# Last layer norm of a four-layer graph network on one Trainium2 core: its scaling on ScalarE, its rows in the ten shared row buffers

## The chip, the cores and the metric

The kernel runs on one core of one Trainium2 chip. A core has a matrix engine (TensorE, PE in the profile), three engines that work element by element (VectorE = DVE, ScalarE = ACT, GpSimd = POOL), a queue engine that issues transfers (SyncE = SP), and 16 DMA engines that move data between the chip's memory and the on-chip memory. The engines run side by side and each takes its own instructions strictly in order; an instruction that has to wait holds back everything behind it on its engine. The metric is the device time of one execution in microseconds; lower is better.

## What is computed

There are 16 graphs of 1024 nodes with 128 features. Four layers follow each other, each of the form `x = layernorm(x + layer(x))`. The change concerns the end of the fourth. That layer is three SAGE convolutions with batch norms, whose three results are concatenated and multiplied by one matrix; the sum with the layer's input is then normalised per node:

```python
xc = jnp.concatenate([h1, h2, h3], axis=-1) * mf[..., None]
return (xc @ Wl + bl) * mf[..., None]
...
m = jnp.mean(x, axis=-1, keepdims=True)
v = jnp.var(x, axis=-1, keepdims=True)
x = (x - m) / jnp.sqrt(v + eps)
```

## The kernel before

Layers 0 to 2 and the preparation of layer 3 take the first 5340 us or so. Their instructions are placed by hand under `tc.manual_schedule`. Layer 3 is written as plain loops over graphs, and the order in which its instructions stand in each engine's queue is chosen by the program's own scheduler: a load can stand in SP's queue well ahead of its place in the source.

Layer 3 has four passes over the 16 graphs, since each batch norm needs the sums over all graphs before the next convolution can be scaled.

- Passes 1 and 2 convolve. `expanded` (L934 to L938) converts a graph's edges from one byte to four, into eight tiles named `m` of 128x1024 numbers each. All `m` tiles share ten buffers (`bufs=10`). The convolution L950 reads them.
- Pass 3 (`second`, then `columns`) makes the third result. `second` (L1089) loads what the convolution left in memory into a tile named `h`, of which there are two buffers. Here the `m` buffers are not used for edges any more.
- Pass 4, the last, is the one that the change touches. It consists of `summed` and the loop behind it.

In pass 4, each tile of a graph holds 512 KB. For graph b, `summed(b)` takes two of the ten `m` buffers and loads the first and second hidden results of the graph into them (L1120); the third still lies on the chip as `R3[b]`. TensorE multiplies the three by the scaled weight (L1125, twelve matmuls of 128x512), and ScalarE moves the sum from PSUM into `o` with the bias added (L1127). The loop calls `summed(b + 1)` before it finishes graph b. To finish graph b, it takes one of the two `h` buffers for `xb` and loads the layer's input rows into it (L1134). TensorE transposes `o` back into rows, four tiles per half graph (L1138); VectorE multiplies by the node mask and adds the input, in place in `xb` (L1140, eight instructions of 128x128). Then comes `layernorm(xb, xb)`:

- VectorE takes the statistics of each of the eight row tiles (L205).
- GpSimd makes the factors from them in ten small instructions (`norm_factors`, L219 to L228; one of them, L227, is a power).
- GpSimd applies them, `x * rs + mean`, in eight instructions of 128x128 (`norm_rows`, L211). (`mean` holds minus the mean times `rs` by then.)

Last, SP issues the store of `xb` to the output (L1143). The load L1134, the loads L1120 and the store L1143 all stand in SP's queue. An `h` buffer is free for the next graph but one when its store has landed.

Layer 0 to 2 have a helper, `norm`, that applies the same factors by ScalarE (L270), so the trace shows that instruction.

Of the kernel before, what the change touches and what calls it, by code (L numbers as in the profile page):

```python
# [29 lines left out]
F32 = mybir.dt.float32  # L30
# [4 lines left out]
AF = mybir.ActivationFunctionType  # L35
# [4 lines left out]
B, N, D, H2 = 16, 1024, 128, 256  # L40
P = 128
T = N // P
# [29 lines left out]
def tile_graph_layers(ctx: ExitStack, tc, a, out):  # L72
    nc = tc.nc
# [5 lines left out]
    small = ctx.enter_context(tc.tile_pool(name="small", bufs=3))  # L79
# [87 lines left out]
    for b in range(B):  # L167
        q, g = divmod(b, G)
        nc.gpsimd.dma_start(out=half_rows[g * R:(g + 1) * R, :, q],
                            in_=a["nodemask"][b].rearrange("(k r) -> r k", r=R))  # L170
# [31 lines left out]
    def layernorm(dst, src):  # L202
        st = small.tile([P, T, 6], F32, name="ln_st")
        for t in range(T):
            nc.vector.bn_stats(out=st[:, t, :], in_=src[:, t, :])  # L205
        norm_rows(dst, src, st)

    def norm_rows(dst, src, st):
        rs, mean = norm_factors(st)
        for t in range(T):  # L210
            nc.gpsimd.tensor_scalar(dst[:, t, :], src[:, t, :], rs[:, t:t + 1], mean[:, t:t + 1],  # L211
                                    op0=ALU.mult, op1=ALU.add)

    def norm_factors(st):

        mv = small.tile([P, 4, T], F32, name="ln_mv")
        mean, apart, var, rs = (mv[:, i, :] for i in range(4))
        gp = nc.gpsimd
        gp.tensor_add(mean, st[:, :, 1], st[:, :, 4])  # L219
        gp.tensor_sub(apart, st[:, :, 1], st[:, :, 4])  # L220
        gp.tensor_scalar(mean, mean, -0.5, 0.0, op0=ALU.mult, op1=ALU.add)
        gp.tensor_mul(apart, apart, apart)
        gp.tensor_add(var, st[:, :, 2], st[:, :, 5])
        gp.tensor_scalar(var, var, 1.0 / D, LN_EPS, op0=ALU.mult, op1=ALU.add)
        gp.tensor_scalar(apart, apart, 0.25, 0.0, op0=ALU.mult, op1=ALU.add)
        gp.tensor_add(var, var, apart)
        gp.tensor_tensor(rs, var, mhalf, op=ALU.pow)  # L227
        gp.tensor_mul(mean, mean, rs)  # L228
        return rs, mean
# [653 lines left out]
    def rows_bank(name):  # L883
        return psum.tile([P, 4, D], F32, tag="subset", name=name, bufs=2)
# [48 lines left out]
    def expanded(near):  # L933
        m = []  # L934
        for c in range(T):
            m.append(sb.tile([P, N], F32R, name="m", bufs=10))
            nc.scalar.copy(m[c], near[:, c, :])  # L937
        return m  # L938
# [129 lines left out]
    sb = ctx.enter_context(tc.tile_pool(name="sb", bufs=1))  # L1068
# [5 lines left out]
    for b in range(B):  # L1074
# [3 lines left out]
        m = expanded(ahead[b][0])  # L1078
# [37 lines left out]
    def summed(b):  # L1116
        hs = []
        for l in range(2):
            r = sb.tile([P, N], F32, name="m", bufs=10)
            nc.sync.dma_start(out=r, in_=hidden[l][b])  # L1120
            hs.append(r)
        p = wide("pl")
        for s in halves:
            for l, r in enumerate((*hs, R3[b])):
                nc.tensor.matmul(p[:, s], scaled[l], r[:, s], start=(l == 0), stop=(l == 2))  # L1125
        o = sb.tile([P, N], F32, name="o", tag="sq", bufs=2)
        nc.scalar.activation(o, p, AF.Identity, bias=pl)  # L1127
        return o

    o = summed(0)  # L1130
    for b in range(B):
        following = summed(b + 1) if b + 1 < B else None
        xb = sb.tile([P, T, D], F32, name="h", bufs=2)
        nc.sync.dma_start(out=xb, in_=x3[b])  # L1134
        for h in range(2):
            p = rows_bank("pback")
            for t in range(4):
                nc.tensor.transpose(p[:, t, :], o[:, (4 * h + t) * P:(4 * h + t + 1) * P], ident)  # L1138
            for t in range(4):
                nc.vector.scalar_tensor_tensor(xb[:, 4 * h + t, :], p[:, t, :], nm[:, 4 * h + t, b:b + 1],  # L1140
                                               xb[:, 4 * h + t, :], op0=ALU.mult, op1=ALU.add)
        layernorm(xb, xb)
        nc.sync.dma_start(out=out[b].rearrange("(t p) d -> p t d", p=P), in_=xb)  # L1143
        o = following

# [24 lines left out]
```

## Time and profile before

| what | us |
|---|---|
| median of three runs (6604.93 to 6620.51) | 6616.69 |
| the profiled execution | 6613.2 |
| its span, first to last instruction | 6611.5 |
| end of VectorE's batch norm statistics aggregate, the last one ahead of pass 4's sums | 6446.4 |
| first transpose back into rows of pass 4 (L1138) | 6457.2 |
| last store issued (L1143) | 6607.3 |

The profiled execution's time is 1.7 us above its span. The span is counted from the first to the last instruction, and all times with two decimals below are read from it. Pass 4 is only the last 2.4% of the span, so the shares of the whole page say nothing about it: PE 86%, DVE 80%, ACT 56% and POOL 58% are averages over all layers. What counts here is the stretch from about 6452 us on.

A row of a view by time reads: start, duration, engine, line, operation, output from input, shapes, how often; in brackets, how long the engine had been idle before it and what ended the wait. A row of the waits reads: who waited, for whom, total us, times, longest.

### The profile page before, as it was taken

To read this page: it belongs to the slowest core of one execution; us is meant where nothing else is said; L and a number is where in the kernel's file an instruction comes from. 1 tells how busy PE (TensorE), PEld (TensorE's weight loads), DVE (VectorE), ACT (ScalarE), POOL (GpSimd) and SP (SyncE) were. 2 spreads that over 40 slices of the span, in tenths; PEclk is the share of its full clock that TensorE was granted. 3 is DMA by queue.
4 is the path that set the end of the run, shared out by engine and by line. 5 is a ranking of instruction groups with operands and counts; after the bars stand their busy time and mean duration, and the time that the engine had idled before them with its cause. 6 is when DMAs were issued, how large, how long until landed. Compare 5 with 4: busy or idle time off the path is not lost. (4 is left out here: it accounts for less than half of the span.)

```text
span 6611.5 us, 85916 instructions
## 1 busy us (share of the span) xinstructions
PE 5697.7 (86%) x27306; PEld 2883.8 (44%) x27306; DVE 5317.7 (80%) x8130; ACT 3733.9 (56%) x6537; POOL 3844.7 (58%) x11285
## 2 busy tenths in 40 slices
PE   6989898989898989899888898888888768787986
PEld 3434344444444444444444444444443345555643
DVE  3989899999999999999999999999998834444453
ACT  4656566666666666666666656666655523333841
POOL 2675767676767776766666676767676511110126
PEclk8989898989898989898989899999987779888997
DMA  5121212121212121212112212121110156563635
GB/s 37 14 27 22 30 24 36 20 27 26 28 28 27 27 27 26 28 26 31 28 29 30 27 26 27 26 27 28 25 25 9 32 93 120 105 124 102 230 128 166
DMA packets 478381, 317.02 MB, mean 48 GB/s; under 512 B 301162, under 2 KB 429668, under 8 KB 473828
## 3 DMA queue, kind: packets, MB, share of 16 engines
q0 software_dynamic: 105648, 84.20, 14.6%
q1 hardware_dynamic: 367600, 226.13, 11.7%
q8 instruction: 214, 3.51, 0.2%
q10 hardware_dynamic: 4676, 1.19, 0.1%
q14 instruction: 243, 1.99, 0.1%
HBM read 412.71 MB, written 117.18 MB: 80 GB/s over the span
## 5 line engine op out<-in xcount | busy, mean ns | idle before, releaser
L831 DVE TENSOR_TENSOR best<-best,pg 128x1024 f32<-128x1024 f32 x2720 | 3234.4, 1210 | 309.0 <-PE pg L779 300.5
L749 ACT ACTIVATE hot<-pm,one_less 128x512 fp32r<-128x512 f32 x2752 | 1882.3, 688 | 1115.1 <-PE pm L748 1102.9
L779 PE MATMUL pg<-hot,high 64*128 64x512 f32 x5504 | 1479.1, 534 | 453.6 <-DVE best L831 417.8
L779 PE MATMUL pg<-hot,low 64*128 64x512 f32 x5504 | 1173.3, 423 | 0.0
L748 PE MATMUL pm<-AT,lit 120*128 120x512 fp8e4 x2752 | 1143.8, 416 | 9.3 <-ACT hot L749 6.2
L779 PEld LDWEIGHTS pg<-hot,high 64*128 64x128 f32 x5504 | 547.9, 196 | 1265.1 <-DVE best L831 792.4
L616 POOL TENSOR_SCALAR sc<-low_counts,half_mask,rest 16x1 f32<-16x1 f32 x992 | 435.7, 439 | 399.6 <-DVE rest L603 305.8
L779 PEld LDWEIGHTS pg<-hot,low 64*128 64x128 f32 x5504 | 573.4, 205 | 0.0
L748 PEld LDWEIGHTS <-lit 120*128 120x128 fp8e4 x2752 | 274.5, 100 | 624.8 <-issue 560.8
L621 POOL TENSOR_SCALAR sc<-sc 16x1 f32<-16x1 f32 x992 | 430.1, 434 | 105.0
L770 ACT CAST low<-pt 128x256 fp32r<-128x256 f32 x688 | 255.6, 371 | 396.3 <-PE pt L768 392.1
L980 POOL TENSOR_TENSOR length<-length,mhalf 128x8 f32<-128x8 f32 x48 | 78.9, 1644 | 571.7 <-DVE length L979 571.7
L618 POOL TENSOR_SCALAR sc<-sc 16x1 f32<-16x1 f32 x992 | 341.8, 345 | 107.7
L624 POOL TENSOR_SCALAR last_rank<-V,sc 16x31 f32<-16x31 bf16 (+30 forms) x992 | 387.1, 390 | 0.0
L623 POOL TENSOR_SCALAR hit<-V,sc 16x31 bf16<-16x31 bf16 (+30 forms) x992 | 372.5, 376 | 0.0
L768 PE MATMUL pt<-high,less 128*128 128x256 f32 x688 | 303.2, 441 | 66.3 <-ACT high L763 58.9
L467 DVE TENSOR_TENSOR sub<-sub,q 128x24 f32<-128x24 f32 (+11 forms) x768 | 306.6, 400 | 24.6 <-ACT q L289 10.5
L619 POOL TENSOR_SCALAR sc<-sc 16x1 f32<-16x1 f32 x992 | 270.1, 272 | 83.3
L937 ACT CAST m<-near 128x1024 fp32r<-128x1024 fp8e4 x256 | 253.3, 1044 | 112.7 <-DVE near L906 59.8
L760 PE MATMUL pt<-ident,sub 128*128 128x128 f32 x1376 | 293.9, 298 | 24.7 <-ACT hot L749 22.0
L377 PE MATMUL pav<-v,eT 128*128 128x128 f32 x2048 | 307.6, 296 | 2.1 <-ACT eT L370 2.1
L617 POOL TENSOR_SCALAR sc<-sc 16x1 f32<-16x1 f32 x992 | 256.6, 259 | 86.6
(258 smaller groups left out, 9495.7 us busy)
## 6 DMA issues: line engine op xcount, KB each, us to landing
removed<-gone SPq DMA_DIRECT2D x128, 256.0 KB
An<-in_adj_dram POOLq DMA_DIRECT2D x16, 1024.0 KB, 15.1
E<-in_adj_dram POOLq DMA_DIRECT2D x128, 128.0 KB, 6.8
gone_all<-removed POOLq DMA_DIRECT2D x64, 256.0 KB, 12.1
near<-in_adjT_dram POOLq DMA_DIRECT2D x16, 1024.0 KB, 17.3
h<-x SPq DMA_DIRECT2D x32, 512.0 KB
kept<-near SPq DMA_DIRECT2D x16, 1024.0 KB
share<-share SPq DMA_DIRECT2D x32, 512.0 KB
```

The costliest lines, as they stand in the source:

```text
L377: nc.tensor.matmul(pav, eT[:, c, :], values[b][:, c, :], start=(c == 0), stop=(c == T - 1))
L467: nc.vector.tensor_max(sub[:, :n_g, n:2 * n], sub[:, :n_g, 0:n], qg[:, 2 * g0:2 * g0 + n_g, k:k + 1].to_broadcast([P, n_g, n]))
L616: gp.tensor_scalar(half, mine, half_mask[:, m], rest[:, n:n + 1], op0=ALU.mult, op1=ALU.add)
L618: gp.tensor_scalar(sf, half, 5.5, sf, op0=ALU.is_gt, op1=ALU.mult)
L621: gp.tensor_scalar(to, at, sf, none, op0=ALU.subtract, op1=ALU.subtract)
L623: gp.tensor_scalar(hit[:, n, n + 1:], V[:, n, n + 1:], at, None, op0=ALU.is_equal)
L624: gp.tensor_scalar(last[:, n + 1:], V[:, n, n + 1:], to, None, op0=ALU.is_le)
L748: nc.tensor.matmul(pm, lit[:, r, :], AT[b * (T + 1) + c][:, halves[h]], start=True, stop=True)
L749: nc.scalar.activation(hots[s][:, halves[h]], pm, AF.Relu, bias=one_less)
L768: nc.tensor.matmul(pt, less, high, start=False, stop=True, skip_group_check=True)
L779: nc.tensor.matmul(pg[:, a], part[rows, at * P:(at + 1) * P], hots[s][rows, halves[h]], start=(k == 0), stop=(k == 1))
L831: nc.vector.tensor_max(own, own, pg)
```

## The change

The rows of a graph, `xb`, come from the ten buffers that `m` tiles use, under the name `xb`, in place of the two that `h` tiles use. In the last layer norm the statistics (VectorE) and the factors (GpSimd) stay as they are, and the eight instructions that apply the factors go from GpSimd to ScalarE, with the same arithmetic. The number of buffers and the memory they take are the same as before. Pass 3 keeps the two `h` buffers for itself.

```diff
     for b in range(B):
         following = summed(b + 1) if b + 1 < B else None
-        xb = sb.tile([P, T, D], F32, name="h", bufs=2)
+        xb = sb.tile([P, T, D], F32, name="xb", tag="m", bufs=10)
         nc.sync.dma_start(out=xb, in_=x3[b])
 ...
-        layernorm(xb, xb)
+        st = small.tile([P, T, 6], F32, name="ln_st")
+        for t in range(T):
+            nc.vector.bn_stats(out=st[:, t, :], in_=xb[:, t, :])
+        rs, mean = norm_factors(st)
+        for t in range(T):
+            nc.scalar.activation(xb[:, t, :], xb[:, t, :], AF.Identity, bias=mean[:, t:t + 1], scale=rs[:, t:t + 1])
         nc.sync.dma_start(out=out[b].rearrange("(t p) d -> p t d", p=P), in_=xb)
```

## The prediction

> **What bounds the kernel now.** I read the page, found that the change lies in the last 2.4% of the span, and asked for the waits of that stretch alone (6452 us to the end), then the chain of waits inside it.
>
> ```profile
> ACT o L1127 <- PE pl L1125: 116.4, 16, 11.6
> DVE h L1140 <- DMA h<-x: 65.4, 11, 9.2
> POOL ln_mv L219 <- DVE ln_st L205: 43.0, 12, 14.2
> ...
> PE pback L1138 <- DVE h L1140: 31.3, 11, 8.5
> ```
>
> See the second line: VectorE's add L1140 stood still for 65.4 us because the input rows had not come. TensorE waits behind it in turn (last line), since the transposes need the PSUM banks that L1140 empties. Why the rows are late is in the chain that ended last:
>
> ```profile
> 6564.17 3.22 DMA out_dram<-h
> 6567.40 3.43 DMA h<-x
> 6570.95 2.16 DVE h L1140 x8
> 6573.11 1.57 DVE ln_st L205 x8
> ...
> 6576.55 1.64 POOL ln_mv L227
> 6578.27 0.21 POOL ln_mv L228
> 6578.57 3.48 POOL h L211 x8
> 6582.07 3.21 DMA out_dram<-h
> ```
>
> It is a ring. The store of one graph lands (3.2 us), only then is the next load into the same buffer issued (3.4), then come the add (2.16), the statistics (1.57), the factors (6574.75 to 6578.47, about 3.8 with the hand-over), the scaling on GpSimd (3.48) and the store again. From store to store, 6564.17 to 6582.07, that is 17.9 us, and with two buffers two graphs go round in it: 8.95 us a graph. Further forward, where hidden results are still being loaded, the ring is 20.2 us (stores at 6507.17 and 6527.40).
>
> Next I looked for what would bound it without the ring. By time, TensorE's first graphs, which run before the ring closes, show its own pace:
>
> ```profile
> 6457.23 1.04 PE L1138 MATMUL pback<-ident,o 128*128 128x128 f32 x8
> ...
> 6463.26 1.04 PE L1138 MATMUL pback<-ident,o 128*128 128x128 f32 x8
> ...
> 6469.28 1.04 PE L1138 MATMUL pback<-ident,o 128*128 128x128 f32 x8
> ```
>
> Three starts 6.03 and 6.02 us apart: TensorE takes 6.03 us a graph, with no gap between. In the same place GpSimd starts L219 at 6461.66 and, never idle in between, again at 6469.17: 7.51 us a graph, of which the scaling is 3.47. VectorE needs 2.16 + 1.63 = 3.8. For the transfers I took the busy times of the stretch:
>
> ```profile
> 6452.00:6611.50 159.50, 108.75 (x309) 53.63 (x307) 59.46 (x256) 17.82 (x16) 108.28 (x288) 0.81 0.53 172
> ```
>
> The columns are length, busy us of PE, PEld, DVE, ACT, POOL, then the granted clock, the DMA share and GB/s. A share of 0.53 is 84.5 us of full use, for 22 hidden loads, 14 row loads and 16 stores of 512 KB each: 1.63 us a transfer. A graph has four: 6.5 us. ACT has 17.82 us of work in 159.5.
>
> **What the Trainium skill says.** "ScalarE: Activation LUTs", section What ACT_TABLE_LOAD costs, gives 280 + 0.833 N ns for an activation with a pointer as bias, 93 more for each further pointer, and 93 of overlap between neighbours. For N = 128 and two pointers that is 480 ns and a pitch of 387. The same instruction in this trace (L270) has a median of 486 ns and eight take 3.18 us, so the page and the trace agree, and I use the trace:
>
> ```profile
> 5338.50 3.18 ACT L270 ACTIVATE X<-y,ln_mv 128x128 f32<-128x128 f32 x8 [10.64 <-POOL ln_mv L228]
> ```
>
> "DMA: Bandwidth & Descriptors", section Anatomy of one DMA, says that DMA engines don't wait on semaphores; the issuing sequencer does. The trace agrees: SP itself stood 33.9 us in 14 waits of L1134 for stores to land, and everything behind stood with it. "TensorE: Matmul & The Clock Gate", section What's actually happening, says that after some 3.4 us of idleness the matrix clock drops to half. Here the granted clock is 0.55 in 6496 to 6500 after a wait of 3.4 us, and L1125's longest matmul is 1.2 us against a median of 0.59. So the ring also costs TensorE speed, which comes back if the ring goes.
>
> **The change part by part.**
>
> *Rows in the ten buffers.* One graph now takes three of ten buffers (two hidden, one of rows), so ten hold 3.3 graphs, where before the rows stood two graphs deep and the hidden results five. A hidden buffer is held about 5 us while it loads and some 5 us while TensorE works; a row buffer 5 while it loads and about 15 from L1140 to the landed store. That is 2 x 10 + 20 = 40 buffer-us a graph, or 4.0 us a graph with ten: below every other limit. What SP issues moves: L1134 for graph b goes forward past stores and hidden loads in SP's queue, and the hidden loads go back by one to two graphs, since they lose buffers. Each has about 5 us to spare by my count (buffers freed by graph 3's sums at 6468.9 and by graph 0's store near 6472 load graph 6, which TensorE reaches near 6482). Nothing is added in number: 32 + 16 loads and 16 stores, as before. The first x loads waited for pass 3's `h` tiles (7.5 us in two waits); they are needed only at 6457, so that wait's end brings nothing. The edges' work in pass 2 costs nothing more if buffers are handed out in program order; the rival below takes the other case.
>
> *Scaling on ScalarE.* Removed from GpSimd: 8 x 0.448, in a row 3.47 us a graph, which leaves it 7.51 - 3.47 = 4.0. Added to ScalarE: 3.18 to its 1.11 of L1127, 4.3 us a graph, under TensorE's 6.03. The function is the Identity that L1127 uses in the same loop, so no table is changed. The new wait is ScalarE's for L228. Behind it stands L1127 of a later graph, and TensorE's transposes wait for that. L1127 of graph b+2 is ready 6.3 us after the transposes of graph b start; the factors of graph b 0.64 + 2.16 + 1.63 + 3.9 = 8.3 us after. If L1127 stands first, it doesn't wait. If it stands second, it ends at 8.3 + 3.2 + 1.1 = 12.6, just past the 12.06 at which its transposes are due. So I cost it from 0 to 0.6 us a graph and take 0. Alone this part would bring nearly nothing, because 3.18 replaces 3.47 in the ring; alone the buffers would stop at GpSimd's 7.51.
>
> *Sum.* With the ring gone, the late thing is TensorE (6.03) or the transfers (6.5). I take 6.5 throughout. First add at 6457.87 as before, fifteen graphs later 6555.4. From the last add to the end it was 6596.20 to 6611.5 = 15.3 us; ScalarE's shorter row makes it 15.0. Span 6570.4, a gain of 41 us. The profiled execution would go from 6613.2 to 6572; it lay 3.5 below the median shown, so on the median's footing I say 6576.
>
> **The rivals.**
>
> *TensorE's pace alone* (the forecast's own best end): if prefetch spreads the transfers well, 15 x 6.03 = 90.5, gain 48, 6569. For it: the last graphs have nothing left to load.
>
> *Transfers crowd.* In 6480 to 6520 they ran at 247 GB/s with 0.73 share, or 8.5 us a graph, and if that is what SP's queue and landing times allow, ten graphs go at 8.5 and five at 6.03: 115 us, gain 23, 6593. For it: single loads took 4.7 us there against 3.4 later. Against it: that stretch was itself gated by the ring, and for 4 us from 6480 the share was 1.00 at 377 GB/s.
>
> *The buffers don't bring the depth* (the change doesn't do what it says). If loads stand behind stores in SP's queue, the ring stays and holds, say, 2.2 graphs: 17.9 / 2.2 = 8.1 us a graph, gain 17, 6600: inside 0.3%. Against it: before, the queue carried hidden loads five graphs ahead.
>
> *Slower: rows take buffers from the edges.* The rows are in memory since layer 2, so loads could be let in while pass 2 still converts edges, and each buffer held from then on delays one conversion (1.045 us) in each of 16 graphs: 16.7 us a buffer. From the third it outweighs the 41 us; with four it is +26, 6642. For it: ScalarE's conversions already wait 52.8 us for buffers. Against it: the first hidden load starts at 6306.90, after the last conversions got their buffers, and the x loads, equally ready, stayed behind `h` tiles until 6426.87: buffers are handed out in the order of the program.
>
> **How the numbers follow.** Forecast with its better end (6563 to 6584): 0.62. Crowded transfers (6585 to 6598): 0.19. No depth, or ScalarE's order costing as much (6598 to 6625): 0.11. Slower by the edges: 0.08. Range 6563 to 6599, which holds the first two. A measurement can tell some 0.3%, 20 us, from no change; hence faster 0.81, same 0.11, slower 0.08.
>
> **What will show it.** L1140's wait for the row load falls from 65.4 us to under 15. Starts of L1138 lie 6.0 to 6.8 us apart, the granted clock from 6460 to 6550 is above 0.95, the DMA share there near 0.9. POOL's busy time in the pass halves to some 65 us, ACT's rises by 51. The first L1138 stays within 2 us of 6457. I am wrong if L1140 still waits for x, if SP waits for stores ahead of loads, if conversions end later than 6308, or if L1127 queues behind the scaling.

## The result, and the profile after

The changed kernel takes 6568.81 us in the median of four runs (6565.02 to 6573.94), the one before 6615.53 (6604.93 to 6620.51; four runs now, where the table above has three): a ratio of 0.9936, 95% interval 0.9921 to 0.9950, or 47 us less. The profiled execution took 6569.97 us, its span is 6568.2. The forecast was 6576 with a range from 6563 to 6599.

The waits of the last stretch, from 6452 us to the end, in the changed kernel (who waited, for whom, total us, times, longest):

```profile
POOL ln_mv L219 <- DVE ln_st L1144: 50.2, 15, 14.2
ACT xb L1147 <- POOL ln_mv L228: 39.4, 16, 7.0
...
PEld pback L1138 <- ACT o L1127: 16.4, 14, 5.2
DVE xb L1140 <- ACT o L1127: 13.1, 5, 2.8
...
PE pback L1138 <- ACT o L1127: 6.5, 8, 5.0
```

The line that carried the forecast, VectorE's 65.4 us of waiting for input rows, has no successor: L1140 waits for no transfer at all. What is left at the head is idleness of engines that are faster than the pace, with one exception. TensorE's transposes L1138 wait for `o`, which ScalarE makes. So ScalarE is late now and then, although it is busy for 58% of the stretch (67.20 of 116.20 us, below).

How late can be read from the starts by time. TensorE and ScalarE in the changed kernel (start, duration, engine, line, operation, shapes, in brackets the idle time before):

```profile
6520.82 1.10 PE L1138 MATMUL pback<-ident,o 128*128 128x128 f32 x8 [0.18 <-ACT o L1127]
...
6526.91 1.10 PE L1138 MATMUL pback<-ident,o 128*128 128x128 f32 x8
...
6533.41 1.09 PE L1138 MATMUL pback<-ident,o 128*128 128x128 f32 x8 [0.25 <-ACT o L1127]
```

```profile
6529.17 3.19 ACT L1147 ACTIVATE xb<-xb,ln_mv 128x128 f32<-128x128 f32 x8 [2.31 <-POOL ln_mv L228]
6532.26 1.10 ACT L1127 ACTIVATE o<-pl,out_bias 128x1024 f32<-128x1024 f32 x1
```

These starts lie 6.09 and 6.50 us apart; over all fifteen intervals, 6458.29 to 6552.05, the mean is 6.25. Follow one pair. Transposes of graph b start at 6520.82. Add, statistics and factors follow, and ScalarE begins the scaling of graph b at 6529.17, 8.35 us later. Behind the scaling in its queue stands L1127 of graph b+2. Its product was complete at 6527.06, but it starts at 6532.26, and the transposes of b+2 start as it ends. That closes a loop over two graphs: 8.35 + 3.09 + 1.15 = 12.59 us for this pair, and 12.45 to 12.59 for the others, or some 6.25 a graph, where TensorE's own pace is 6.03.

The busy times of the pass, in the changed kernel (length, busy us of PE, PEld, DVE, ACT, POOL, then granted clock, DMA share and GB/s):

```profile
6500.00:6540.00 40.00, 39.40 (x130) 19.26 (x129) 22.45 (x97) 26.94 (x58) 21.42 (x69) 1.00 0.98 326
...
6452.00:6568.20 116.20, 95.52 (x310) 47.51 (x308) 59.35 (x256) 67.20 (x144) 52.70 (x160) 0.91 0.74 244
```

GpSimd went from 108.28 to 52.70 us, ScalarE from 17.82 to 67.20. TensorE does the same matmuls in 13 us less busy time; its granted clock goes from 0.81 to 0.91 over the pass, and from 0.88 to 1.00 between 6460 and 6540. The DMA share reaches 0.98 in the middle, and still nothing waits for a load.

In the comparisons that follow, pass 4 is counted from the first start of L1138 to the end of the span, because the first 6450 us scatter by some 15 us between the profiled executions (the first start of L1138 lies anywhere from 6454 to 6470). In that part the changed kernel was seen to differ only in the loads that SP issues ahead: eight hidden ones instead of ten, and the first two of rows at 6313.83 and 6328.15 instead of from 6426.87 on. The mean interval is that of the 16 starts of L1138. e4, e5, e6 and e8 ran once each.

| kernel | first L1138 | span | pass 4 | mean interval |
|---|---|---|---|---|
| before | 6457.2 | 6611.5 | 154.3 | 8.85 |
| changed | 6458.3 | 6568.2 | 109.9 | 6.25 |
| e1: buffers alone | 6456.4 | 6581.3 | 124.9 | 6.5 (six of 6.03, then about 7.3, the last 1.9) |
| e2: scaling alone | 6454.6 | 6609.4 | 154.8 | 8.7 |
| e3: sum first | 6460.8 | 6564.5 | 103.7 | 6.03 but for the last |
| e4: second power | 6464.9 | 6590.8 | 125.9 | 7.2 |
| e5: ring of three | 6469.8 | 6587.4 | 117.6 | 6.76 |
| e6: less product, sum first | 6468.4 | 6571.5 | 103.1 | 4.3, later 6.8 |
| e8: second power, sum first | 6454.3 | 6561.4 | 107.1 | 6.03 but for the last |

### The profile page after: what moved, and what is told of

Same layout as the page of the kernel before. It is cut to its first block, busy times and chain, and to the rows that moved or that the text cites. A ratio compares the mean times of both kernels' runs of the same rounds, so it can differ in the third digit from the quotient of the medians.

```text
span 6568.2 us, 85836 instructions
## 1 busy us (share of the span) xinstructions
PE 5661.4 (86%) x27177; PEld 2873.0 (44%) x27306; DVE 5317.8 (81%) x8130; ACT 3780.8 (58%) x6665; POOL 3794.2 (58%) x11157
## 3 DMA queue, kind: packets, MB, share of 16 engines
q0 software_dynamic: 105648, 84.20, 14.9%
## 5 line engine op out<-in xcount | busy, mean ns | idle before, releaser
L621 POOL TENSOR_SCALAR sc<-sc 16x1 f32<-16x1 f32 x992 | 425.5, 429 | 105.0
L618 POOL TENSOR_SCALAR sc<-sc 16x1 f32<-16x1 f32 x992 | 351.6, 354 | 107.7
L619 POOL TENSOR_SCALAR sc<-sc 16x1 f32<-16x1 f32 x992 | 269.9, 272 | 83.4
L626 POOL TENSOR_TENSOR low_counts<-low_counts,hit 16x31 f32<-16x31 f32 (+30 forms) x992 | 264.6, 267 | 77.7
```

The costliest lines, as they stand in the source:

```text
L618: gp.tensor_scalar(sf, half, 5.5, sf, op0=ALU.is_gt, op1=ALU.mult)
L621: gp.tensor_scalar(to, at, sf, none, op0=ALU.subtract, op1=ALU.subtract)
```

## Experiments: each half of the change alone

The first, only the buffers, scaling left on GpSimd:

```diff
-        xb = sb.tile([P, T, D], F32, name="h", bufs=2)
+        xb = sb.tile([P, T, D], F32, name="xb", tag="m", bufs=10)
 ...
         layernorm(xb, xb)
```

> Rows in the ten buffers, scaling left on GpSimd. Theory (the ring of two buffers was the bound, and without it the next limit is GpSimd, 4.0 us of factors and 3.5 of scaling): starts of L1138 about 7.5 us apart, GpSimd without gaps, L1140 hardly waiting for its rows; pass 4 is 15 x 7.51 + 0.6 + 15.3 = 128.6 us against 154.3, so some 6590 us. Rival (the buffers bring it all): as the changed kernel, 6569. Rival (the buffers bring nothing by themselves): 6616.

Measured: a ratio of 0.9953 to the kernel before on the same chip, interval 0.9936 to 0.9970, medians 6592.04 and 6623.88 us: 32 us less. GpSimd by time in this kernel:

```profile
6533.54 0.21 POOL L219 TENSOR_TENSOR ln_mv<-ln_st 128x8 f32<-128x8 f32 x1
...
6537.37 3.47 POOL L211 TENSOR_SCALAR xb<-xb,ln_mv 128x128 f32<-128x128 f32 x8
6540.80 0.21 POOL L219 TENSOR_TENSOR ln_mv<-ln_st 128x8 f32<-128x8 f32 x1
...
6544.62 3.47 POOL L211 TENSOR_SCALAR xb<-xb,ln_mv 128x128 f32<-128x128 f32 x8
```

No bracket stands behind any of these rows, nor behind those left out: once it has begun, GpSimd never waits, and begins a graph every 7.26 us, from the first to the last. TensorE ran ahead at 6.03 us for six graphs and then waited for hidden results (8.2 and 6.2 us, for weights and for matmuls, in nine waits each). That buffers come free no faster than GpSimd finishes graphs is the likely reason; it was not tested by itself. So GpSimd was the second limit, as the theory had it, and a little faster than the 7.51 I had taken from two starts of the kernel before. The pass came out 4 us shorter than expected for that reason.

The second, only the scaling:

```diff
         xb = sb.tile([P, T, D], F32, name="h", bufs=2)
 ...
+            nc.scalar.activation(xb[:, t, :], xb[:, t, :], AF.Identity, bias=mean[:, t:t + 1], scale=rs[:, t:t + 1])
```

> Scaling on ScalarE, rows still in two buffers. Theory: the ring stays, one turn is shorter by the 0.3 us between 3.48 and 3.18, seven to eight turns, so 2 us: some 6613, and L1140 still waits some 60 us for its rows. Rival (GpSimd's load was the limit): as the changed kernel, 6569. Rival (each half brings half): 6592.

Measured: a ratio of 0.9998, interval 0.9990 to 1.0007. The waits of its pass, from 6452 us on:

```profile
POOL ln_mv L219 <- DVE ln_st L1144: 97.8, 16, 14.1
ACT h L1147 <- POOL ln_mv L228: 71.5, 16, 8.6
DVE h L1140 <- DMA h<-x: 56.7, 10, 10.7
```

The third line is the ring, still there. GpSimd was given 55 us of leisure and spent it waiting; nothing was gained, not even the 2 us that were expected. The two halves bring 32 us and nothing, and together 47: the second half is worth its 15 us only where the first has made GpSimd the bound.

## Experiments: what sets the 6.25 us

In e3, the loop of graph b hands its tile and factors on, and the next turn issues the scaling behind `summed(b + 2)`. The kernel's `behind` keeps ScalarE's queue in that order.

```diff
+    def scale_and_store(b, xb, rs, mean):
+        for t in range(T):
+            nc.scalar.activation(xb[:, t, :], xb[:, t, :], AF.Identity, bias=mean[:, t:t + 1], scale=rs[:, t:t + 1])
+        nc.sync.dma_start(out=out[b].rearrange("(t p) d -> p t d", p=P), in_=xb)
 ...
         following = summed(b + 1) if b + 1 < B else None
+        if waiting is not None:
+            start = len(nc.cur_bb.bb.instructions)
+            scale_and_store(*waiting)
+            if following is not None:
+                behind(nc.cur_bb.bb.instructions[start - 1], start)
 ...
+        waiting = (b, xb, *norm_factors(st))
         o = following
+    scale_and_store(*waiting)
```

> The changed kernel with ScalarE's queue in the other order: the bias and move of graph b+2 (o) ahead of the scaling of graph b. Theory (the 6.25 us a graph come from a loop of two graphs, transposes to add to statistics to factors to scaling to o to transposes, 12.5 us long): starts of L1138 6.03 us apart and all alike, 15 x 0.22 = 3.3 us less than the changed kernel, 6565.5. Rival (the transfers, at a share of 0.98, set the 6.25): intervals stay 6.2 to 6.3 with TensorE waiting for hidden results, time as the changed kernel, 6569.

Measured: a ratio of 0.9924 to the kernel before, interval 0.9909 to 0.9939. TensorE by time:

```profile
6533.11 1.04 PE L1148 MATMUL pback<-ident,o 128*128 128x128 f32 x8
...
6539.14 1.04 PE L1148 MATMUL pback<-ident,o 128*128 128x128 f32 x8
...
6545.17 1.04 PE L1148 MATMUL pback<-ident,o 128*128 128x128 f32 x8
...
6547.13 0.63 PE L1148 MATMUL pback<-ident,o 128*128 128x128 f32 x4 [0.93 <-DVE xb L1150]
```

The transposes (now L1148) start every 6.02 to 6.03 us; the loop is gone. SP's queue differs little, and TensorE waits for no load in either kernel, so the gain does not come from there. The rival, that the transfers set 6.25, falls with it, although the DMA engines are busy all the time in e3:

```profile
6500.00:6540.00 40.00, 40.00 (x136) 20.77 (x135) 23.74 (x104) 28.74 (x62) 21.76 (x69) 1.00 1.00 349
```

A DMA share of 1.00 over 40 us, and TensorE busy in all 40 of them. The pass is 6.2 us shorter than in the changed kernel, not 3.3. The rest is at the end: the last transposes no longer wait for a scaling (4.98 us of TensorE's waits in the changed kernel) but follow 2 us behind the ones before.

The other way round, e4 makes the supposed loop longer, on an engine that has room:

```diff
-        gp.tensor_tensor(rs, var, mhalf, op=ALU.pow)
+        for _ in range(powers): gp.tensor_tensor(rs, var, mhalf, op=ALU.pow)
 ...
-        rs, mean = norm_factors(st)
+        rs, mean = norm_factors(st, 2)
```

> The changed kernel with the power L227 computed twice in the last layer norm: 1.65 us more on GpSimd, which has room (4.0 of 6.25 us a graph). Theory (loop of two graphs through ScalarE's queue): a pair of starts of L1138 goes from 12.5 to 14.15 us, 7.08 a graph, and the time rises by 14 x 0.82 = 11 us plus 1.65 at the end. Rival (TensorE or the transfers set the pace, and the chain beside them has slack): intervals stay 6.25, and only the 1.65 us at the end are added.

In its trace the starts of L1138 pair off:

```profile
6501.15 1.10 PE L1138 MATMUL pback<-ident,o 128*128 128x128 f32 x8 [1.54 <-ACT o L1127]
...
6507.61 1.09 PE L1138 MATMUL pback<-ident,o 128*128 128x128 f32 x8 [0.22 <-ACT o L1127]
...
6515.40 1.09 PE L1138 MATMUL pback<-ident,o 128*128 128x128 f32 x8 [1.54 <-ACT o L1127]
...
6521.88 1.09 PE L1138 MATMUL pback<-ident,o 128*128 128x128 f32 x8 [0.23 <-ACT o L1127]
```

From 6501.15 to 6515.40 a pair takes 14.25 us; the theory said 14.15. The pass grew by 16.0 us, where 11 plus 1.65 were expected: the first pair was drawn out by 3.4 us, the other six by 1.7 to 2.0, and the end by 1.8. One more instruction of 1.65 us a graph, 26 us of work in all, on an engine that even then is busy for 63% of the pass (79.05 of 125.9 us), cost 16 us.

And e8 puts the same second power into the order of e3.

> The second power of e4 in the order of e3. Theory (the power cost time only through the loop in ScalarE's queue): starts of L1138 stay 6.03 us apart, pass 4 is as long as in e3 (103.7 us from the first start of L1138 to the end) plus 1.65 us at the end. Rival (GpSimd's longer work delays the stores, and with them buffers and loads): intervals above 6.2 us, TensorE waiting for hidden results.

TensorE by time, at the end:

```profile
6532.63 1.04 PE L1148 MATMUL pback<-ident,o 128*128 128x128 f32 x8
...
6538.66 1.04 PE L1148 MATMUL pback<-ident,o 128*128 128x128 f32 x8
...
6540.84 1.38 PE L1148 MATMUL pback<-ident,o 128*128 128x128 f32 x8 [1.15 <-ACT o L1127]
```

The starts stay 6.02 to 6.03 us apart, from 6454.30 to 6538.66. The pass is 107.1 us, 3.4 more than in e3, where 1.65 were expected. That is twice 1.65: the last two graphs come 2 us apart, so GpSimd does their factors one behind the other (from 6543.21 to 6553.97 without a pause), and both extra powers lie in the tail. In this order the power is hidden but at the end.

## Experiments: what is left of the ring and of the transfers

e5 keeps ScalarE's scaling and all ten `m` buffers for the hidden results, and gives the rows a ring of three:

```diff
-        xb = sb.tile([P, T, D], F32, name="xb", tag="m", bufs=10)
+        xb = sb.tile([P, T, D], F32, name="h", bufs=2) if b % 3 < 2 else sb.tile([P, T, D], F32, name="share")
```

> Scaling on ScalarE as in the changed kernel, but the rows go round three buffers of their own (the two h buffers and the one of the share tile, idle in pass 4), and all ten m buffers stay with the hidden results. Theory (only the number of row buffers counts, a turn of 17.6 to 20 us shared by the graphs in it): three graphs to a turn, 5.9 to 6.7 us a graph, so starts of L1138 some 6.3 to 6.6 us apart, L1140's wait for rows under 20 us instead of 65, pass 4 about 112 us. Rival (one more buffer is not enough because the store and the load are further apart under crowding): 7.5 us or more a graph, 130 us.

The wait of L1140 for rows is 13.3 us, as expected (7.0 for `h`, 6.3 for `share`), but the mean interval is 6.76 and the pass 117.6 us, worse than forecast by 6. SP's own waits in this kernel point to a reason:

```profile
SPq L1134 <- DMA out_dram<-h: 20.4, 8, 4.0
...
SPq L1134 <- DMA out_dram<-share: 9.7, 4, 3.0
```

SP stood 30 us for stores to land, ahead of row loads, with all later loads and stores behind it in the queue. The same tile's turn, from store to store, took 20.5, 18.9 and 23.3 us (`share`, stores at 6493.77, 6514.23, 6533.15, 6556.43), of which a third is 6.3 to 7.8. So three buffers take away most of the wait, and the turn itself does not stay at the length it had. That SP's waits lengthen the turn is read from the order of its queue; no run tests it by itself, and the loop through ScalarE's queue is still in this kernel too. In the changed kernel the row loads wait for no store; its hidden loads do, for 12.9 us in all.

e6 asks how far the transfers are from being the bound. It takes the order of e3 and leaves out part of the product, not of the loads:

```diff
-        for s in halves:
-            for l, r in enumerate((*hs, R3[b])):
-                nc.tensor.matmul(p[:, s], scaled[l], r[:, s], start=(l == 0), stop=(l == 2))
+        for h, s in enumerate(halves):
+            for l, r in ((h, hs[h]), (2, R3[b])):
+                nc.tensor.matmul(p[:, s], scaled[l], r[:, s], start=(l < 2), stop=(l == 2))
```

> The order of e3 (o before scaling), with the product of each half graph leaving out one of the two hidden results (4 of 12 matmuls a graph; all loads stay), so TensorE needs 4.3 us a graph, ScalarE 4.3, GpSimd 4.0, VectorE 3.8. Theory (the transfers are the next limit, 1.59 us each): the first graphs some 4.3 to 4.5 us apart, then, once what was loaded ahead is used, about 6.4 us a graph with TensorE waiting for hidden results; the last start of L1138 near 78 us after the first, DMA share 0.95 or more in between. Rival (the transfers have room to spare): 4.3 to 4.6 us a graph throughout, 66 us from first to last.

The first six graphs came 4.31 us apart, and then:

```profile
6522.57 1.10 PE L1125 MATMUL pl<-m,Wl_s 128*128 128x512 f32 x2 [0.75 <-DMA m<-hidden]
...
6527.51 1.09 PE L1148 MATMUL pback<-ident,o 128*128 128x128 f32 x8 [1.27 <-DVE ln_st L1154]
6529.34 1.10 PE L1125 MATMUL pl<-m,Wl_s 128*128 128x512 f32 x2 [0.73 <-DMA m<-hidden]
...
6534.27 1.10 PE L1148 MATMUL pback<-ident,o 128*128 128x128 f32 x8 [1.27 <-ACT o L1127]
```

From 6520.73 to 6554.54 the mean is 6.76 us, with TensorE waiting for hidden results in every graph, and 86 us lie between the first start and the last (78 expected). The share was 0.87 from 6500 to 6540, not 0.95. SP's queue in the same stretch, and the product that follows:

```profile
6530.56 0.39 SPq L1133 DMA_DIRECT2D out_dram<-xb  x1
6531.04 1.70 SPq L1120 DMA_DIRECT2D m<-hidden  x2
...
6535.93 1.10 PE L1125 MATMUL pl<-m,Wl_s 128*128 128x512 f32 x2 [0.56 <-DMA m<-hidden]
```

Read by time, this closes another loop over two graphs. L1127 moves the sum of the product that begins at 6522.57, and starts at 6526.34. The scaling (L1132 here) stands behind it and begins at 6527.35. The store waits for the scaling, the hidden loads stand behind the store, and the next product but one begins when they have landed, 13.36 us after the first, or 6.7 a graph. The hidden loads take 4.8 us of it. By the trace they also take a buffer that a product frees at about the time at which the store is issued, and busy DMA engines may make their landing slower. Which of these sets the 6.76 was not separated. The outcome is clear all the same. A third of TensorE's product less, and the pass is 0.6 us shorter than in e3: behind TensorE another limit stands close. That it is the DMA engines themselves is not shown. At e3's 349 GB/s the four transfers of a graph take 6.0 us (an estimate, 4 x 512 KB by that rate), so there they just keep up with TensorE's 6.03.

## The order against the changed kernel

Since e3 beats the changed kernel by 6 us in the traces and a single time scatters by about as much, both ran once more on one chip.

> The changed kernel once more, on the same chip as the next run, for the comparison of the two: ratio to the kernel before 0.9936 as in its own measurement, interval within 0.992 to 0.995; pass 4 from the first start of L1138 to the end 110 us, pairs of starts 12.5 us apart.

> The order of e3 once more, beside the changed kernel. By the traces pass 4 is 103.7 us against 109.9, so theory (the order is worth 6 us): a ratio 0.0009 below the changed kernel's, 0.9927 if that is at 0.9936; the scatter of a run, some 5 us to either side, may hide it. Rival (the difference of the two traces was the chance of one execution): equal ratios, and starts of L1138 in this trace no longer 6.03 us apart.

| kernel | median us | ratio to before | interval |
|---|---|---|---|
| changed, again | 6571.10 | 0.9929 | 0.9916 to 0.9943 |
| sum first, again | 6565.86 | 0.9920 | 0.9906 to 0.9933 |

The ratios differ by 0.0009, as expected, and the medians by 5.2 us, but the intervals overlap, so by time alone this isn't settled. The traces repeat to a tenth of a microsecond: pass 4 is 110.0 and 103.7 us, pairs of starts 12.5 us in the one, and 6.02 or 6.03 us for every start but the last in the other. By the traces the order is worth 6 us, and e3's order is the best version found.

## Why the prediction was right

*The ring was the bound: shown.* L1140's 65.4 us of waiting for rows fell to nothing, and e1, which takes away the ring alone, brings 32 of the 47 us. e2 shows that moving the scaling from GpSimd to ScalarE, 3.18 us for 3.48, leaves the ring as it was.

*The second half needs the first: shown.* The prediction had the buffers alone stop at GpSimd's pace and the scaling alone bring nearly nothing; e1 and e2 say 32 us and none.

*The pace of 6.5 us: the mis-sized term.* The prediction divided 84.5 us of DMA use by 52 transfers and let that set the pace. The measured pace is 6.25, and 15 x 0.25 = 3.7 us of the difference come from here. Three things were wrong in it. The pace was not set by transfers: e3 ran at 6.03 with the share at 1.00. The price of a transfer was too high as well, since 172 GB/s at a share of 0.53 stands for some 325 at full use (an estimate, the one divided by the other), and e3 moved 349. And the wait that did set it, L1127 behind the scaling, was priced "from 0 to 0.6 us a graph" and then taken as 0; it is 0.22. The prediction even had its length, "12.6, just past the 12.06", and did not go on to see that the two numbers close a loop. That the sum came out so near is in part luck: one limit was priced too high and the other at nothing, and the two errors have opposite signs.

*Its signs of being wrong.* One of the four came true in full: L1127 does queue behind the scaling. It costs 0.22 us a graph, so the time stayed in the range. SP also waits for stores ahead of loads, 12.9 us in all, but of hidden loads only, and TensorE waits for none of them; L1140 does not wait for `x`. For the fourth see the slower rival below.

*The tail: right.* 15.0 us expected from the last add to the end; it is 14.9 (6553.26 to 6568.2).

*The sum.* 41 us expected; the pass is 44.4 shorter, so that 41 + 3.7 accounts for it. The profiled executions differ by 43 and the medians by 47, within what the first 6450 us scatter.

*TensorE's clock: right in the number.* The prediction took from "TensorE: Matmul & The Clock Gate", section What's actually happening, that idleness halves the clock and expected the loss to return. The granted clock is 1.00 from 6460 to 6540, where it was 0.88 before. But e2 has 0.98 there, with the ring in place and no time gained: a higher clock alone brought nothing.

*The slower rival: out.* The last conversion of edges starts at 6307.7 and ends at 6308.7, a microsecond later than in the kernel before and past the 6308 that the prediction had set as a sign. But the first load of rows into the ten buffers is issued only at 6313.83, and the conversions wait for buffers 53.7 us against 53.0. Rows took no buffer from the edges; the front of this execution was late by 0.4 us already at 5339.

*A slip.* GpSimd's busy time was to fall to "some 65 us"; 108.3 - 55.5 is 52.8, and 52.7 was measured.

## What to carry to other kernels

Where a store must land before the next load into its buffer, add up the whole turn and divide by the buffers; if that exceeds every engine's own pace, more depth is the first thing to buy; before that, moving a step of the turn to another engine at much the same length brought nothing here (e2). The turn itself may grow with the depth (e5). When work moves to an engine with time to spare, what counts is the place it gets in that engine's queue: follow what stands behind it until the chain comes back to its start, and divide the loop by the graphs that are in it. Price such a wait as a loop, not as a delay that is sometimes hidden.

## What the runs showed that I had not expected

The 16 DMA engines can be at a share of 1.00 for 40 us, moving 349 GB/s in transfers of 512 KB, while the consumer never waits (e3). In the kernel before, the same transfers went at 247 GB/s and 0.73 from 6480 to 6500, single loads of rows landed after up to 4.7 us, and VectorE waited for them. High DMA use said nothing about who waited. Nor is the share a rate: at 1.00 it went with 349 GB/s here and with 377 for 4 us in the kernel before.

The front of the kernel, 6450 us long and all but unchanged, ended up to 15 us apart between profiled executions, while pass 4 repeated to 0.1 us in the two kernels that were profiled twice (the changed one and e3). For a change in a short last stage, the stage's own length in the trace is the sharper measure.
